# Small PSUM tiles for the attention's projections, constants as a scheduled job, and one engine for W z, in a convolution, attention and recurrence kernel

## The chip, the cores and the metric

The kernel runs on one core of a Trainium2 chip. The core has a matrix engine (TensorE, PE in the profile; PEld is its weight load), VectorE (DVE), ScalarE (ACT), GpSimd (POOL) and SyncE (SP), whose queue issues most of the transfers. The metric is the device time of one execution in microseconds, as the median of the runs shown.

## What is computed

The input x is 32 images of 128 channels and 64 x 64 pixels, all in 32-bit floats. Cut to what matters:

```python
x = x + dyn_conv3x3(group_norm(x))           # per image a kernel, mixed of four by softmax(sigmoid(.))
t = tokens(x)                                # (32, 4096, 128)
t = t + L1_attn(layer_norm(t))
t = t + L1_ffn(layer_norm(t))

def L1_attn(x):                              # windows of 144 tokens, stride 72, 4 heads of 4
    xb = x @ w_down.T + b_down               # 128 -> 16
    q, k, v = split(windows(xb) @ in_proj_w.T + in_proj_b)
    o = softmax(q @ k.T / 2) @ v @ out_proj_w.T + out_proj_b
    up = overlap_average(o) @ w_up.T + b_up  # 16 -> 128
    return layer_norm(x + sigmoid(gate) * up) * gamma + beta

def L1_ffn(x):
    z = batch_norm(x @ W.T)                  # over all images and tokens
    y[t] = sigmoid(z[t] + y[t - 1] @ V.T)    # a scan over 4096 tokens
    return y
```

## The kernel before

The program has two long stages. **The images** (`images`, up to L1150) take the 32 images through convolution, attention and the product with W. **The runs** (`by_runs`, L1603) do the scan.

The runs come only after the last image, since the normalisation of z takes its mean and variance over all of them. The scan of 4096 tokens is cut into 128 runs of 32 steps (RUN), and each run starts 20 steps early (WARM) from zero. Two images make a group, so one step works on 128 x 256 numbers. The 16 groups go through four streams in turn: a step is a product of `fVT` with the last y on PE into one of eight PSUM tiles `v`, the addition of scl times z, a sigmoid on ACT with the shift, and a copy of y into the place of z on POOL. `product` (L1632) does the addition in two ways. For five of six step numbers VectorE adds scl z to the PSUM tile (L1636); for the sixth PE multiplies z by the diagonal matrix `dgs` into the same tile first (L1638, L1639). A finished group is added onto the output in memory by a transfer that POOL issues (L1667), and then the load of the group six further on can follow, where its buffer is the same.

In the images, an order of work is written out when the program is built. Each image has eight generators (jobs): load, conv, project, feed, attend, divide in two halves, and tail. A job yields before each step with the engine that the step begins on, the PSUM pool that it needs, and the tiles that it reads. A planner (L1127) keeps a modelled clock for each engine and takes the first job, by due time, whose next step can begin no later than PE is free; if there is none, the one that can begin first. Convolution comes last in this order whatever its due time, so it fills what the others leave. Every engine then runs its own instructions strictly in the order written. The clock of the model is not the chip's; it only sets the order.

- load (L620): an image and its statistics; mixes the four kernels `k_d` by way of buffers `kx` into `wb`. The frames hold two images.
- conv (L698): transforms rows on POOL and VectorE (`ut`), multiplies on PE into `nm` tiles, and VectorE adds them to the frame.
- project (L753): layer norm into `zt`, and the down projection to 16 numbers per token: 32 matmuls into one `sc` tile, drained by one ACT instruction to `xb`, transposed by VectorE to `gt`.
- feed (L823): queries, keys and values from `gt`: qs and ks through one `sc` tile, Vc and VT through another. It waits until attention of the image before has read them all ("sets").
- attend (L888): 14 sets of windows, each in two halves; scores into an `sc` tile, exponentials by ACT, and the weighted sums of the half before into the tile `av`.
- divide (L996): sends the sums of the exponentials through small transfers to a layout in which VectorE inverts them (`cd`) and back; multiplies by `spr` on PE into an `sc` tile to spread them to all rows, scales `av`, and adds the up projection (`wc`) to `zt`. It runs for windows 0 to 3 and then for the rest.
- tail (L1066): the two layer norms and the product with W, and stores z.

[...] one `sc` tile of four banks, three `nm` tiles of one bank each, and one for `av`. A job that wants `sc` waits until whoever had it has drained all of it.

Ahead of the planner, the constants of the attention are made in a row: 52 small loads on SP, fills on POOL, copies on VectorE, and products on PE with `wuT` and others through `nm` tiles (L404 to L508). Before them come the loads of images 0 and 1 (L361) and the conversion of the four kernels to `k_d`.

Of the kernel before, what the change touches and what calls it, by code (L numbers as in the profile page):

```python
# [8 lines left out]
F32 = mybir.dt.float32  # L9
# [4 lines left out]
P = 128  # L14
EPS = 1e-5
H = W = 64
T = H * W
# [171 lines left out]
def hybrid_kernel(  # L189
# [153 lines left out]
    def images(nc):  # L343
# [6 lines left out]
        with ExitStack() as pa:  # L350
# [10 lines left out]
            for b in range(NF):  # L361
                fetch(b)


            with tc.tile_pool(name="gk", bufs=2) as gk:
                for k in range(NK):
# [11 lines left out]
                    nc.sync.dma_start(k_d[k], g4)  # L378
            keep = pa.enter_context(tc.tile_pool(name="keep", bufs=1))
# [23 lines left out]

            wqkv = []  # L404
            for i, n in enumerate(("wqB", "wkB", "wvB")):
                t = kept([P, P], n, 0.0)
                for g in range(NQ):
                    r = slice(16 * g, 16 * g + 16)
                    nc.sync.dma_start(t[r, r], in_projT[:, i * DK : (i + 1) * DK])
                wqkv.append(t)  # L410
            wqB, wkB, wvB = wqkv
            bqB, bkB = kept([P, 1], "bqB"), kept([P, 1], "bkB")
            bd = kept([P, 1], "bd", 0.0)
            wd2 = kept([P, 48], "wd2", 0.0)
            nc.vector.tensor_copy(wd2[:, DK : 2 * DK], wd[:, 0:DK])
            in_b1 = in_proj_b.rearrange("(c o) -> c o", o=1)
            for g in range(NQ):
                r = slice(16 * g, 16 * g + 16)
                nc.sync.dma_start(bqB[r], in_b1[0:DK])
                nc.sync.dma_start(bkB[r], in_b1[DK : 2 * DK])  # L420
            for g in range(NQ):
                nc.sync.dma_start(
                    bd[16 * g : 16 * g + DK], b_down.rearrange("(c o) -> c o", o=1)
                )

            mqk = kept([P, 2 * NH], "mqk")
            nc.vector.tensor_reduce(
                mqk, memb.rearrange("p (q g) -> p g q", q=4), axis=AX.X, op=ALU.add
            )

            m16 = kept([P, 8], "m16")
            nc.vector.tensor_reduce(
                m16, ident.rearrange("p (g k) -> p g k", k=16), axis=AX.X, op=ALU.add
            )
            mvt = kept([P, 2 * NH, HD], "mvt")
            nc.vector.tensor_copy(mvt, m16.rearrange("p (g o) -> p g o", o=1).to_broadcast([P, 2 * NH, HD]))

            VEs = []
            for i in range(2):
                v = kept([P, 4 * NH * NR + 32 - NR], f"VE{i}", 0.0)  # L440
                for h in range(NH):
                    nc.gpsimd.memset(
                        v[:, 0 : 4 * NH * NR].rearrange("p (q h o) -> p q h o", q=4, h=NH)[:, :, h, DK + h], 1.0
                    )
                VEs.append(v)
            Vc = kept([P, NWG * NQ * DK], "Vc")
            VTf = kept([P, NWG * NQ * NR + 32 - NR], "VT", 0.0)
            VT = VTf[:, 0 : NWG * NQ * NR].rearrange("p (w o) -> p w o", o=NR)
            for q in range(4):
                for u in range(2):  # L450
                    for m in range(NWG):
                        nc.vector.tensor_copy(
                            VT[:, NQ * m + 2 * q + u, DK:NR], mvt[:, NH * u : NH * (u + 1), 0]
                        )

            aw = kept([DK, NR], "aw")
            nc.sync.dma_start(aw[:, 0:DK], out_proj_w)
            bv = kept([DK, NH, HD], "bv")  # L460
            nc.sync.dma_start(
# [291 lines left out]
            def project(b):  # L753

                while ("conv", b) not in done:
                    yield
# [1039 lines left out]
```

## Time and profile before

| | us |
|---|---|
| median of 3 runs (lowest, highest) | 5605.47 (5600.29, 5619.85) |
| profiled execution, its time | 5616.06 |
| its span | 5614.3 |
| PE busy in the span | 4826.9 (86%) |
| DVE busy | 3636.3 (65%) |
| ACT busy | 2391.4 (43%) |
| POOL busy | 1606.5 (29%) |
| first matmul of a convolution | at 101 |
| last one | at 4664 |
| first step of the runs | at 4985 |

The span is the time from the first to the last instruction of one execution; the execution's own time is a little more. The page cuts the span into 40 slices and gives each engine's busy share in tenths (9 is 90% or more) and the granted PE clock:

```profile
PE   2897889989899898988988989989889897659996
DVE  4665666676666766766666766666676665347774
PEclk9998999999999999999999999999999999869998
```

PE is near full from the second slice on, falls off for two slices near the end of the images, and is full again in the runs, where VectorE and ACT are at seven tenths. A group row of the page has the line, engine, operation, tiles and shape, the number of instructions, and then busy time, mean length of one, and the engine's idle time before them with what ended it. Most of the images' instructions carry one line (L173), that of the wrapper which notes each operation for the model; so they are told apart by their tiles.

### The profile page before, as it was taken

The page shows a single profiled execution, that of the slowest core. Times are in us where ns is not written, and L with a number is a line of the kernel's source. Part 1 is how long each engine was busy: PE and PEld are TensorE (multiplying, and loading weights), DVE is VectorE, ACT ScalarE, POOL GpSimd, SP SyncE. Part 2 cuts the span into 40 slices and gives each one's busy share as a digit, 9 for nine tenths or more (in the row PEclk, how much of TensorE's full clock was granted, in tenths as well). Part 3 has the DMA queues.
Part 4 walks back from the last instruction along what each step waited for, and adds up shares of the span by engine and source line. Part 5 has one row for each costly group of instructions (what it writes and reads, how often), then busy time and mean ns, then how long its engine had stood idle before and what let it go on. Part 6 is the DMA issues. An engine that isn't in the chain of part 4 may idle for free. (4 is left out here: it accounts for less than half of the span.)

```text
span 5614.3 us, 105560 instructions
## 1 busy us (share of the span) xinstructions
PE 4826.9 (86%) x43707; PEld 2388.9 (43%) x43707; DVE 3636.3 (65%) x5044; ACT 2391.4 (43%) x3564; POOL 1606.5 (29%) x1561
## 2 busy tenths in 40 slices
PE   2897889989899898988988989989889897659996
PEld 1443444444444444444444444444444443326663
DVE  4665666676666766766666766666676665347774
ACT  0243444444344444434434433434444444327774
POOL 1331322222232222322322222222222221105664
PEclk9998999999999999999999999999999999869998
DMA  4534444454545545454444544544554444355997
GB/s 107 159 110 136 146 146 147 154 164 147 159 146 162 161 134 160 142 166 154 143 156 128 171 138 147 157 158 146 161 162 140 154 143 146 113 226 145 254 232 149
DMA packets 456796, 866.13 MB, mean 154 GB/s; under 512 B 297312, under 2 KB 307824, under 8 KB 423536
## 3 DMA queue, kind: packets, MB, share of 16 engines
q1 hardware_dynamic: 447600, 792.12, 44.3%
q0 software_dynamic: 8704, 67.11, 5.9%
q8 instruction: 350, 5.73, 0.4%
q14 instruction: 142, 1.16, 0.1%
HBM read 575.10 MB, written 275.78 MB: 152 GB/s over the span
## 5 line engine op out<-in xcount | busy, mean ns | idle before, releaser
L173 PE MATMUL nm<-ut,wb 128*128 128x512 f32 x3072 | 1599.6, 641 | 13.6 <-DVE wb L173 13.3
L173 ACT ACTIVATE ex<-sc 128x1152 f32<-128x1152 f32 x896 | 1013.6, 1131 | 1259.0 <-PE sc L173 1252.0
L173 PE MATMUL sc<-qe,ks 32*128 32x288 f32 x7168 | 722.5, 473 | 328.8 <-ACT ext L173 91.9
L173 POOL TENSOR_TENSOR qe<-qs,mqk 128x576 f32<-128x576 f32 x448 | 626.8, 1405 | 1316.2 <-PE sc L173 1292.3
L173 PEld LDWEIGHTS nm<-ut,wb 128*128 128x128 f32 x3072 | 538.2, 196 | 597.4 <-issue 584.8
L173 POOL TENSOR_TENSOR ut<-frames 128x576 f32<-128x576 f32 x384 | 538.9, 1433 | 870.1 <-PE nm L173 840.9
L173 DVE TENSOR_TENSOR frames<-frames,nm 128x512 f32<-128x512 f32 (+1 forms) x640 | 494.6, 791 | 290.1 <-PE nm L173 282.9
L173 PEld LDWEIGHTS sc<-qe,ks 32*128 32x128 f32 x7168 | 296.7, 190 | 875.4 <-issue 315.1
L173 PE MATMUL av<-ex,VE 128*32 128x144 f32 x14336 | 653.1, 302 | 2.6 <-DVE av L173 1.5
L173 PEld LDWEIGHTS av<-ex,VE 128*32 128x32 f32 x14336 | 372.2, 112 | 337.4 <-issue 269.3
L1635 PE MATMUL v<-yw,fVT 128*128 128x256 f32 (+1 forms) x1368 | 389.5, 417 | 73.3 <-ACT yw L1654 27.3
L1636 DVE SCALAR_TENSOR_TENSOR v<-zr,scl,v 128x256 f32<-128x256 f32 (+1 forms) x557 | 333.7, 654 | 138.3 <-PE v L1635 137.1
L173 DVE TENSOR_TENSOR zt<-zt,place 128x1024 f32<-128x1024 f32 x256 | 331.8, 1296 | 115.5 <-DMA place<-r_d 99.6
L173 DVE SCALAR_TENSOR_TENSOR wb<-kx,co,wb 128x768 f32<-128x768 f32 x192 | 243.3, 1267 | 141.9 <-DMA kx<-k_d 140.2
L1635 PEld LDWEIGHTS v<-yw,fVT 128*128 128x128 f32 x1368 | 234.2, 194 | 215.6 <-ACT yw L1663 96.8
L173 ACT ACTIVATE place<-zt 128x1024 f32<-128x1024 f32 x256 | 263.7, 1052 | 129.8 <-DVE zt L173 87.4
L173 DVE TENSOR_TENSOR place<-place 128x256 f32<-128x256 f32 x416 | 229.6, 552 | 137.5 <-ACT place L173 128.1
L1664 POOL COPY zr<-yw 128x256 f32<-128x256 f32 x416 | 261.4, 694 | 159.9 <-ACT yw L1663 159.7
L1663 ACT ACTIVATE yw<-v,shf 128x256 f32<-128x256 f32 x512 | 241.5, 475 | 129.8 <-DVE v L1636 67.3
L173 PE MATMUL nm<-place,avg 128*32 128x256 f32 x3072 | 250.4, 399 | 17.0 <-ACT place L173 15.2
L173 ACT COPY zt<-nm 128x512 f32<-128x512 f32 x256 | 150.1, 587 | 267.8 <-PE nm L173 267.7
L173 DVE SCALAR_TENSOR_TENSOR zt<-sc,gbc,zt 128x576 f32<-128x576 f32 (+1 forms) x192 | 175.4, 913 | 135.5 <-PE sc L173 135.3
(194 smaller groups left out, 5664.6 us busy)
## 6 DMA issues: line engine op xcount, KB each, us to landing
place<-r_d SPq DMA_DIRECT2D x512, 512.0 KB
kx<-k_d SPq DMA_DIRECT2D x256, 384.0 KB
x_d<-frames SPq DMA_DIRECT2D x32, 2112.0 KB
place<-x_d SPq DMA_DIRECT2D x128, 528.0 KB
frames<-in_x_dram SPq DMA_DIRECT2D x128, 512.0 KB
out_dram<-zt SPq DMA_DIRECT2D x64, 1024.0 KB
z_d<-zt SPq DMA_DIRECT2D x64, 1024.0 KB
zr<-z_d SPq DMA_DIRECT2D x26, 2048.0 KB
```

Of the source, the lines that this page charges most:

```text
L173: got = f(*args, **kw)
L1635: nc.tensor.matmul(ps, fVT, y, start=True, stop=True)
L1636: nc.vector.scalar_tensor_tensor(ps, z, scl, ps, ALU.mult, ALU.add)
L1663: nc.scalar.activation(yw[r % 2], ps, AF.Sigmoid, bias=shf)
L1664: nc.gpsimd.tensor_copy(zt[:, :, :, r], yw[r % 2])
```

## The change

- The down projection takes four `nm` tiles in turn, each drained by an ACT instruction of its own.
- Feed works in three parts, of windows 0 to 2, 3 to 5 and 6. Each part takes four `nm` tiles (q, k, values, values of the last 16 tokens) and starts when attention of the image before is past its windows. Attention starts after the first part and waits for the others at sets 6 and 12. `qs`, `ks` and `kt` get fixed places.
- The inverse sums take an `nm` tile for each of their three or two parts.
- Attention's wait for the second divide of the image before comes ahead of the set's copies instead of behind.
- The constants become a job of the planner with due time 0.5, which project waits for; image 1 is fetched behind the kernels' conversion.
- Due times: second divide from b - 0.15 to b + 0.6, project from b - 1.4 to b - 1.25, load from b - 2.8 to b - 2.5, feed from b - 1.2 to b - 0.9.
- In the runs every product is a matmul and a VectorE addition; `dgs` is gone.

```diff
@@ -358,8 +358,7 @@
                 for i in range(4):
                     nc.sync.dma_start(rows(xs[b % NF], 16 * i, 16), x[b, :, 16 * i : 16 * i + 16, :])
 
-            for b in range(NF):
-                fetch(b)
+            fetch(0)
 
 
             with tc.tile_pool(name="gk", bufs=2) as gk:
@@ -376,6 +375,8 @@
                     nc.vector.tensor_add(g4[:, 1], g4[:, 1], g3[:, :, 1])
                     nc.vector.tensor_scalar_mul(g4[:, 1:3], g4[:, 1:3], 0.5)
                     nc.sync.dma_start(k_d[k], g4)
+            for b in range(1, NF):
+                fetch(b)
             keep = pa.enter_context(tc.tile_pool(name="keep", bufs=1))
...
-            wqkv = []
-            for i, n in enumerate(("wqB", "wkB", "wvB")):
-                t = kept([P, P], n, 0.0)
...
+            wqB = wkB = wvB = bqB = bkB = bd = wd2 = mqk = mvt = VEs = Vc = VTf = VT = wc = fWc = gbc = avg = spr = None
...
             def project(b):
 
-                while ("conv", b) not in done:
+                while ("conv", b) not in done or "setup" not in done:
                     yield
                 xt = done["conv", b]
...
-                yield "PE", "sc", (zt[:, 0:T],)
 
                 xb = one.tile([P, 2, 4 * WIN], F32, name="xb")
-                ps = sc_tile()
                 for k in range(4):
                     n = 2 * WIN if k % 2 == 0 else WIN
+                    yield "PE", "nm", (zt[:, 0:T],)
+                    ps = nm_tile()
                     for v in range(2):
                         for q in range(4):
                             o = base[q] + GT * (k // 2) + 2 * WIN * (k % 2) + 4 * WIN * v
                             w = n if v else 2 * WIN
                             nc.tensor.matmul(
-                                ps[32 * q : 32 * q + 32, k, 0:w],
+                                ps[32 * q : 32 * q + 32, 0:w],
                                 wd2[:, DK * (1 - v) : DK * (3 - v)],
                                 zt[:, o : o + w],
                                 start=(v == 0),
                                 stop=(v == 1),
                             )
-                nc.scalar.activation(
-                    xb.rearrange("p u (k t) -> p (u k) t", k=2),
-                    ps[:, :, 0 : 2 * WIN],
-                    AF.Identity,
-                    bias=bd,
-                )
+                    nc.scalar.activation(
+                        xb.rearrange("p u (k t) -> p (u k) t", k=2)[:, k], ps[:, 0 : 2 * WIN], AF.Identity, bias=bd
+                    )
                 yield "DVE", None, (xb,)
...
-                done["gt", b] = zt, gt, gf, gtt
+                done["gt", b] = zt, gf, gtt
+            qs, ks = kept([P, GT], "qs"), kept([P, GT], "ks")
+            kt = kept([P, NWG, 2 * NH, 16], "kt")
 
             def feed(b):
 
-                while ("gt", b) not in done or (b and ("sets", b - 1) not in done):
-                    yield
-                zt, gt, gf, gtt = done["gt", b]
-                yield "PE", "sc", (gt,)
-                qs = one.tile([P, GT], F32, name="qs")
-                ks = one.tile([P, GT], F32, name="ks")
-                ps = sc_tile()
-                for i, wt in enumerate((wqB, wkB)):
-                    for c in range(2):
-                        n = 32 - c
+                for m0, m1 in ((0, 3), (3, 6), (6, NWG)):
+                    while ("gt", b) not in done or (
+                        b and (gone.get(("att", b - 1), 0) <= 4 * m1 if m1 < NWG else ("sets", b - 1) not in done)
+                    ):
+                        yield
+                    zt, gf, gtt = done["gt", b]
+                    t, n = slice(WIN * m0, WIN * m1), m1 - m0
+                    for wt in (wqB, wkB):
+                        yield "PE", "nm", (gf,)
+                        ps = nm_tile()[:, 0 : WIN * n]
+                        nc.tensor.matmul(ps, wt, gf[:, t], start=True, stop=True)
+                        if wt is wqB:
+                            nc.scalar.activation(
+                                qs[:, t].rearrange("p (m d r) -> p m d r", m=n, r=9),
+                                ps.rearrange("p (m r d) -> p m d r", m=n, r=9),
+                                AF.Identity,
+                                bias=bqB,
+                            )
+                        else:
+                            nc.scalar.activation(ks[:, t], ps, AF.Identity, bias=bkB)
+                    nc.gpsimd.tensor_mul(
+                        kt[:, m0:m1],
+                        ks[:, t].rearrange("p (m o t) -> p m o t", o=1, t=WIN)[:, :, :, P:WIN].to_broadcast(
+                            [P, n, 2 * NH, 16]
+                        ),
+                        mqk.rearrange("p (m g o) -> p m g o", m=1, o=1).to_broadcast([P, n, 2 * NH, 16]),
+                    )
+                    yield "PE", "nm", (gf,)
+                    ps = nm_tile()
+                    for m in range(m0, m1):
                         nc.tensor.matmul(
-                            ps[:, 2 * i + c, 0 : 16 * n],
-                            wt,
-                            gf[:, BLK * c : BLK * c + 16 * n],
+                            ps[:, P * (m - m0) : P * (m - m0 + 1)],
+                            gf[:, WIN * m : WIN * m + P],
+                            wvB,
                             start=True,
                             stop=True,
                         )
...
-                done["proj", b] = zt, qs, ks, kt
+                    nc.scalar.copy(Vc[:, P * m0 : P * m1], ps[:, 0 : P * n])
+                    yield "PE", "nm", (gtt,)
+                    ps = nm_tile()
+                    for m in range(m0, m1):
+                        nc.tensor.matmul(
+                            ps[:, P * (m - m0) : P * (m - m0 + 1)],
+                            gtt[:, m].rearrange("p g k -> p (g k)"),
+                            wvB,
+                            start=True,
+                            stop=True,
+                        )
+                    nc.vector.tensor_mul(
+                        VT[:, NQ * m0 : NQ * m1].rearrange("p (w u) o -> p w u o", u=2)[:, :, :, 0:DK],
+                        ps[:, 0 : P * n].rearrange("p (w u o) -> p w u o", u=2, o=DK),
+                        mvt.rearrange("p (w u h) f -> p w u (h f)", w=1, u=2).to_broadcast([P, n * 4, 2, DK]),
+                    )
+                    done["fed", b, m0] = True
+                done["proj", b] = zt
 
             av = kept([P, 2 * GT], "av")
 
             def attend(b):
 
-                while ("proj", b) not in done or (b and ("div", b - 1, 0) not in done):
+                while ("fed", b, 0) not in done or (
+                    b and (("sets", b - 1) not in done or ("div", b - 1, 0) not in done)
+                ):
                     yield
-                zt, qs, ks, kt = done["proj", b]
+                zt = done["gt", b][0]
...
                 for s in range(2 * NWG):
                     m, u = s // 2, s % 2
+                    while (b and s == 10 and ("div", b - 1, 1) not in done) or (
+                        s in (6, 12) and ("fed", b, m) not in done
+                    ):
+                        yield
                     o = m * WIN
                     v0 = VEs[s % 2]
...
-                    while b and s == 10 and ("div", b - 1, 1) not in done:
-                        yield
...
                         held = (s, ap, hp, ex, ext)
+                        gone["att", b] = 2 * s + hp + 1
...
-                yield "PE", "sc", (av[:, t],)
-                ps = sc_tile()
                 parts = 3 - d
                 n = n // parts
                 for c in range(parts):
                     o = slice(2 * WIN * m0 + n * c, 2 * WIN * m0 + n * (c + 1))
+                    yield "PE", "nm", (av[:, o],)
+                    ps = nm_tile()
                     for q in range(4):
                         r = slice(32 * q, 32 * q + NR + NH)
-                        nc.tensor.matmul(
-                            ps[32 * q : 32 * q + 32, c, 0:n], spr[r], av[r, o], start=True, stop=True
-                        )
-                av2 = av[:, t].rearrange("p (c t) -> p c t", c=parts)
-                nc.vector.tensor_mul(av2, av2, ps[:, 0:parts, 0:n])
+                        nc.tensor.matmul(ps[32 * q : 32 * q + 32, 0:n], spr[r], av[r, o], start=True, stop=True)
+                    nc.vector.tensor_mul(av[:, o], av[:, o], ps[:, 0:n])
...
-                zt = done["proj", b][0]
+                zt = done["proj", b]
...
+            def setup():
+                nonlocal wqB, wkB, wvB, bqB, bkB, bd, wd2, mqk, mvt, VEs, Vc, VTf, VT, wc, fWc, gbc, avg, spr
+                yield "SP", None, ()
+                wqkv = []
...
+                yield "DVE", None, (bv, aw)
+                nc.vector.tensor_mul(bv, bv, aw[:, 0:DK].rearrange("e (h f) -> e h f", f=HD))
...
+                yield "DVE", None, (bo, aw)
+                nc.vector.tensor_add(aw[:, DK : DK + 1], aw[:, DK : DK + 1], bo)
...
+                yield "PE", "nm", (aw, wuT)
+                wps = nm_tile()
+                wmn = kept([P, 1], "wmn")
+                for q in range(4):
+                    r = slice(32 * q, 32 * q + NR)
+                    nc.tensor.matmul(wps[r, 0:P], aw, wuT, start=True, stop=True)
+                    nc.vector.tensor_reduce(wmn[r], wps[r, 0:P], axis=AX.X, op=ALU.add)
+                    nc.vector.tensor_scalar_mul(wmn[r], wmn[r], 1.0 / P)
+                    nc.vector.tensor_scalar(
+                        wc[r], wps[r, 0:P], wmn[r], ghalf[r], ALU.subtract, ALU.mult
+                    )
+                yield "PE", "nm", ()
+                fcp = nm_tile()
...
+                done["setup"] = True
+            done, gone = {}, {}
             pa.enter_context(tc.manual_schedule())
-            jobs = []
+            jobs = [[False, 0.5, 0, setup(), None]]
             for b in range(NB):
                 for stage, g in enumerate(
                     (tail(b), divide(b, 0), divide(b, 1), attend(b), project(b), load(b), conv(b), feed(b))
                 ):
-                    jobs.append([stage == 6, b + (-0.05, -0.15, -0.15, 1.65, -1.4, -2.8, 0, -1.2)[stage], b, g, None])
+                    jobs.append([stage == 6, b + (-0.05, -0.15, 0.6, 1.65, -1.25, -2.5, 0, -0.9)[stage], b, g, None])
...
-            dg = hp.tile([P, P], F32, name="dgs")
-            nc.vector.tensor_scalar_mul(dg, ident, scl)
...
-            def product(ps, z, y, n):
-                if n % 6:
-                    nc.tensor.matmul(ps, fVT, y, start=True, stop=True)
-                    nc.vector.scalar_tensor_tensor(ps, z, scl, ps, ALU.mult, ALU.add)
-                else:
-                    nc.tensor.matmul(ps, dg, z, start=True, stop=False)
-                    nc.tensor.matmul(ps, fVT, y, start=False, stop=True)
 
...
-                            product(ps, z, yw[1 - r % 2][:, :, 1:], r + j)
+                            nc.tensor.matmul(ps, fVT, yw[1 - r % 2][:, :, 1:], start=True, stop=True)
+                            nc.vector.scalar_tensor_tensor(ps, z, scl, ps, ALU.mult, ALU.add)
                             nc.scalar.activation(y, ps, AF.Sigmoid, bias=shf)
                         yield
                     for r in range(RUN):
                         ps = p_v.tile([P, NI, NRUN], F32, name=f"v{j}")
-                        product(ps, zt[:, :, :, r], yw[1 - r % 2], r + j)
+                        nc.tensor.matmul(ps, fVT, yw[1 - r % 2], start=True, stop=True)
+                        nc.vector.scalar_tensor_tensor(
+                            ps, zt[:, :, :, r], scl, ps, ALU.mult, ALU.add
+                        )
                         nc.scalar.activation(yw[r % 2], ps, AF.Sigmoid, bias=shf)
                         nc.gpsimd.tensor_copy(zt[:, :, :, r], yw[r % 2])
                         yield
```

## The prediction

> **What bounds it.** I read the 40 slices first, then busy time by stage, then one stage at a time. The columns of the stage table are stretch, length, busy time of PE, PEld, DVE, ACT and POOL (instructions), granted clock, DMA share, GB/s.
>
> ```profile
> 101.00:400.00 299.00, 270.88 (x2134) 129.28 (x2138) 196.95 (x264) 89.11 (x123) 91.87 (x75) 0.96 0.39 119
> 400.00:4600.00 4200.00, 3741.84 (x36823) 1789.21 (x36820) 2815.72 (x3673) 1756.65 (x2396) 1119.93 (x871) 0.95 0.49 152
> 4600.00:4985.00 385.00, 255.55 (x2834) 124.86 (x2833) 181.22 (x238) 148.55 (x199) 46.16 (x38) 0.84 0.37 131
> 5034.00:5520.00 486.00, 473.64 (x1713) 302.28 (x1712) 360.99 (x648) 350.40 (x751) 297.28 (x484) 1.00 0.77 198
> ```
>
> PE bounds both long stages: 89% busy in the images (400 to 4600) and 97% in the runs (5034 to 5520). It hardly works before 101 us, and the last images (4600 to 4985) have too little for it. In the images only the 458 us of PE idle can be won. The PE groups there, the last field being idle time before them:
>
> ```profile
> L173 PE MATMUL nm<-ut,wb 128*128 128x512 f32 x2679 | 1411.6, 644 | 0.0
> L173 PE MATMUL sc<-qe,ks 32*128 32x288 f32 x6336 | 636.9, 472 | 280.7 <-ACT ext L173 76.4 <-POOL qe L173 60.8 <-ACT ex L173 49.7
> L173 PE MATMUL sc<-av,spr 24*32 24x384 f32 (+1 forms) x1144 | 163.1, 566 | 60.8 <-DMA av<-cd 59.1 <-ACT ex L173 1.6
> L173 PE MATMUL sc<-wvB,gt 128*128 128x128 f32 x392 | 56.7, 304 | 13.1 <-ACT ks L173 13.1
> L173 PE MATMUL nm<-mv,grp 128*128 128x1 f32 x56 | 12.6, 295 | 41.6 <-DVE mv L173 41.6
> ```
>
> The convolution never waits for a buffer (0.0), so where it is at hand it fills every hole; the idle time lies where attention runs without it.
>
> **Start, -14 us.** SyncE's queue (start, length, what):
>
> ```profile
> 53.33 0.32 SPq L378 DMA_DIRECT2D k_d<-g  x1
> ...
> 80.46 0.42 SPq L173 DMA_DIRECT2D wuT<-in_w_upT_dram  x1
> 94.71 4.59 SPq L173 DMA_DIRECT2D kx<-k_d  x3
> ```
>
> The 52 constant loads take SP from 56.7 to 80.9. PE then waits for wuT until 82.6, and the first image's statistics queue behind it: kx only goes on at 94.7, and the convolution is steady from 109.8. After the change the four fetches of image 1 (half of 16.6 us, 8.3) go behind the kernels, so SP's sum is the same and ends near 81. But the job gives way before its PE work, so the statistics (mv was ready at 27) are done by then, and kx follows at once: 94.7 - 80.9 = 14 saved. Bounds: 0 if the job's PE steps still come first; 38 if its loads fall behind all kx. The job issues its loads in one step ahead of kernel 2, so I take the 14. Its 60-odd DVE instructions (the VT copies take 4.1 us) and POOL fills fall into the time before k_d is written. Its four up-projection matmuls, each waiting some 1.9 us for DVE, now lie in that wait; uncovered they cost 6.
>
> **Images, -75 us.** The edits take 5 of 39 sc uses per image (down 1, feed 2, spr 2) to the nm tiles: 4 + 12 + 5 = 21 uses. The matmul columns stay the same. The order of due times within one turn was feed, both divides, tail, load, project; it becomes first divide, tail, feed, load, second divide, project. PE waits that belong to the moved drains: ks 13.1, and DVE VT (15.5 by the waits table) before the next scores: both go, 29. For the inverse sums PE waits 59.1 for the DMA, 17 times; nm doesn't bring the DMA sooner, but the second divide's later due time puts it, with the eight small transfers that it issues on SP (2.75 and 2.85 us per four), behind tail, feed and load; the tail of that image then starts later by about as much. I take half, 30; bounds 0 and 59. Feed now runs inside the previous attention. Before, qs, ks, kt on POOL, Vc and VT stood in a row, here 9.2 us from qs to the first exponential (timeline of one turn):
>
> ```profile
> 2712.64 1.10 ACT L173 ACTIVATE qs<-sc,bqB 128x1008 f32<-128x1008 f32 x1 [4.95 <-PE sc L173]
> ...
> 2721.83 1.13 ACT L173 ACTIVATE ex<-sc 128x1152 f32<-128x1152 f32 x1 [2.31 <-PE sc L173]
> ```
>
> What is late next there is project, which had gt only at 2881 for the following image, so the chain shortens in about two images of three. PE's share of this is the POOL qe wait, 60.8, of which half lies at the starts of images: 30. Sum 89.
>
> Added: ACT splits 1 to 4 and three times 1 to 3, 9 instructions more. ACT's copies of 64 and 512 columns (237, 587 ns) give 0.78 ns a column and 0.19 us fixed, so 1.7 us per image; DVE gains 5 (VT 2, spr 3) at about 0.17 and POOL 2, some 1 us each. All lie on engines 42%, 67% and 27% busy beside PE; uncovered they would cost 3.7 us x 32 = 118. Here a rule speaks against the change: **the Trainium skill**, Perfetto Trace Analysis, "Optimizing Scalar/DVE Operations", says that each ACT or DVE instruction has a fixed access cost and that larger operations pay when the engine is saturated. It gives ACT 51 ns on PSUM, 0.5 us per image instead of 1.7; ACT is not saturated, so neither figure reaches the end. The price that can reach PE is a late release of nm: 0.0 us over the convolution's 16 uses per image, but 9.3 us over 8 product uses in 28 images, 0.04 each. Half of that: 21 x 0.02 x 32 = 14. Net -75; bounds +80 (rival C) and -229 (half the idle). The wait for the second divide at s = 10, put ahead of VE and qe, holds up those two on ACT and POOL, then the scores behind them; the divide is done within 20 us of the previous attention's end, long before s = 10: nothing.
>
> **Last images, -9 us.** Nothing fills here: image 31's gt comes at 4783, its first exponential at 4803. A third of the feed is enough to start: some 5 us instead of 14.
>
> **Runs, -43 us.** One round (16 groups make four) is 131.85 us and 204 products. Its row by stage, DVE back to back, PE back to back in the chain of waits, and products with W z on PE:
>
> ```profile
> 5103.95:5235.80 131.85, 129.54 (x475) 84.10 (x474) 98.86 (x180) 96.91 (x209) 83.56 (x136) 1.00 0.90 229
> ```
> ```profile
> 5122.39 9.13 DVE L1636 SCALAR_TENSOR_TENSOR v<-zr,scl,v 128x256 f32<-128x256 f32 x16 [0.77 <-PE v L1635]
> ```
> ```profile
> 5087.43 9.15 PE v L1635 x34
> ```
> ```profile
> 5201.15 1.03 PE L1638 MATMUL v<-zr,dgs 128*128 128x256 f32 x2
> 5201.99 0.61 PE L1639 MATMUL v<-yw,fVT 128*128 128x256 f32 x2
> 5202.44 1.03 PE L1638 MATMUL v<-zr,dgs 128*128 128x256 f32 x2
> ```
>
> A product with dgs takes PE 5202.44 - 5201.15 = 1.29 us, a plain one 9.15/17 = 0.54 (34 records, two for each product). 170 x 0.54 + 34 x 1.29 = 136, about the round. After: PE at most 204 x 0.54 = 110; DVE's pitch is (9.13 - 0.65)/15 = 0.565, so 204 x 0.565 = 115 and DVE is the bound. The same page of the skill would give DVE 125 ns on PSUM beside 256 columns at 0.96 GHz (VectorE: DVE Perf Modes, "Specifications"): 0.39, 80 us a round, and -110 for the stage. The row decides, and at 97% busy a round is 119. A lone stream takes 2.46 us a step at half clock, under 2.0 at full clock: 52 steps are 104, below 119. DMA:
>
> ```profile
> q0 software_dynamic: 2176, 16.78, 63.2%
> q1 hardware_dynamic: 908, 13.30, 26.1%
> ```
>
> A store takes 0.632 x 131.85/4 = 20.8 us, a load about 10: 31 per group against 29.8. A group's store and the load that waits for it must end two groups later, at 60 us. Over ten loads they fall 12 us behind, with 60 - 31 = 29 to spare, so DMA doesn't bind. Saved: 12.9 x 486/131.85 = 48. Where one or two streams run alone, a dgs step took 1.77 us instead of 2.46, without DVE; some seven of those come back: +5.
>
> **Sum.** -14 - 75 - 9 - 43 = -141. The profiled execution took 5616.06 (span 5614.3): 5475. The median of the runs is 10.6 lower: 5605.47 - 141 = 5464, say 5465.
>
> **Rivals.** A, the images stay (25%): conv fills what the feed leaves, and the PE waits move instead of going; for it, 89% busy PE; against it, 29 us of waits lose their cause. -66, 5540. B, the images gain more (16%): attention without gaps halves the 458 idle; for it, attentions of 113 to 127 us in a period of 149 us (qs rows of images 6 to 29); against it, 41.6 us waits for mv, untouched. -229 - 66: 5310. C, slower (6%): the nm tiles become the wait. Three serve convolution, product, deviations and now 21 uses more, drained by in-order DVE and ACT; at the deviations' 0.34 us a use (12.5 + 1.4 + 15.0 over 3 uses in 28 images) that is 228 us against 89 + 66 gained: +73, 5680. It decides from 0.23 us a use; the 0.0 of the convolution speaks against it. D, DVE takes its full 0.65 us per product (8%): 133 a round, runs +10 instead of -43: 5518. The 16 in a row speak against it. My forecast keeps 45%.
>
> **How the numbers follow.** Its own range is 5420 to 5520; A and D reach to 5560, B down to 5360 for part of its chance: 5360 to 5570. A measurement tells apart about 0.3%, 17 us. Faster: forecast, A, B and D less 3%: 0.91; slower: C, 0.06; same 0.03.
>
> **What would show it.** Convolution steady near 95 us; no PE wait for ks or VT; the scores' idle time below 240; "nm<-ut,wb" still near 0.0; rounds of 119 us with DVE at 97% and PE near 85%. Wrong if PE waits at nm, if attention's gaps stay near 30 us, or if a round is over 128.

## The result, and the profile after

| | before | after |
|---|---|---|
| median (lowest, highest), us | 5604.6 (5600.29, 5619.85) | 5547.35 (5532.06, 5552.78) |
| ratio, 95% interval | | 0.9889 [0.9862, 0.9916] |
| profiled execution, its span | 5616.06, 5614.3 | 5545.78, 5544.0 |
| first convolution matmul at | 101 | 92 |
| from there to the last one | 4563 | 4570 |
| from there to the first step of the runs | 324 | 295 |
| the runs | 627 | 587 |

The change takes off 57 us, not 141. By the traces (70 us between the spans) the start gives 9, the convolution part -7, the last images 29 and the runs 40. The runs are counted from the first sigmoid on. Both image terms together are 22 where the prediction had 84.

The slices of the page after, in tenths:

```profile
PE   3898888979989889898898988998988988749995
DVE  5656765666766667676676666676666765448995
PEclk9998999989999999999999999999999999869997
```

The middle looks as before. Only the runs, the last slices, show a change: VectorE is now full there. The stages, with columns as in the prediction:

```profile
101.00:400.00 299.00, 276.95 (x2259) 132.31 (x2259) 181.12 (x257) 99.33 (x150) 92.26 (x79) 0.93 0.34 102
400.00:4600.00 4200.00, 3741.42 (x36926) 1799.82 (x36928) 2780.42 (x3845) 1804.58 (x2649) 1085.39 (x929) 0.95 0.49 153
5080.00:5180.00 100.00, 98.07 (x352) 52.78 (x352) 99.16 (x183) 84.47 (x179) 69.93 (x116) 1.00 0.96 248
5180.00:5280.00 100.00, 95.37 (x341) 50.93 (x340) 96.95 (x178) 82.29 (x175) 69.98 (x115) 1.00 1.03 283
```

From 400 to 4600, PE is busy 3741.42 us against 3741.84: as idle as before. What it waits for is not the same. PE groups after, 400 to 4600, the last field being the idle time:

```profile
L173 PE MATMUL nm<-ut,wb 128*128 128x512 f32 x2714 | 1389.9, 633 | 9.7 <-DVE wb L173 9.0
L173 PE MATMUL sc<-qe,ks 32*128 32x288 f32 x6300 | 631.7, 471 | 204.4 <-ACT ext L173 81.5 <-ACT VE L173 64.8 <-POOL qe L173 34.9
L173 PE MATMUL av<-ex,VE 128*32 128x144 f32 x12592 | 570.3, 301 | 21.8 <-DVE av L173 21.8
L173 PE MATMUL nm<-place,avg 128*32 128x256 f32 x2720 | 215.0, 394 | 34.7 <-ACT place L173 33.9
L173 PE MATMUL nm<-av,spr 24*32 24x384 f32 (+1 forms) x1144 | 164.2, 589 | 134.6 <-DMA av<-cd 134.4
L173 PE MATMUL nm<-wvB,gt 128*128 128x128 f32 x392 | 66.3, 300 | 9.2 <-ACT qs L173 7.1 <-ACT ks L173 1.4
L173 PE MATMUL nm<-zt,avg 128*32 128x256 f32 x928 | 65.8, 400 | 24.7 <-DVE zt L173 24.7
L173 PE MATMUL nm<-mv,grp 128*128 128x1 f32 x56 | 11.0, 265 | 0.0
```

Gone are the waits for ks and VT (29), for mv (41.6) and 26 of the 60.8 for qe; the scores' idle time fell from 280.7 to 204.4. Some 12 us come back in feed, where the next matmul now waits until ACT or VectorE has drained an `nm` tile (8.8 of it for qs; the row of `wvB,gt` has 9.2). New are 75 us at the inverse sums (59.1 to 134.4), and some 54 at `av`, `place` and `zt`. The one large loser is the wait for `av<-cd`, which the prediction had put on the winning side.

What stands there is read from SyncE's queue and from PE, here around the second divide of image 10. SyncE sends `av`'s sums out (`cd<-av`, here at 1815.72) and the inverses back (`av<-cd`). Its queue after (start, length, what; the last number counts the transfers in the row):

```profile
1836.06 0.32 SPq L173 DMA_DIRECT2D z_d<-zt  x1
1836.48 9.53 SPq L173 DMA_DIRECT2D frames<-in_x_dram  x4
1846.06 2.82 SPq L173 DMA_DIRECT2D kx<-k_d  x2
1848.99 3.02 SPq L173 DMA_DIRECT2D av<-cd  x4
```

PE after, in the same stretch:

```profile
1843.17 0.70 PE L173 MATMUL av<-ex,VE 128*32 128x144 f32 x16
1843.68 0.43 PE L173 MATMUL av<-ext,VT 128*32 128x144 f32 x8
1853.84 3.59 PE L173 MATMUL nm<-av,spr 24*32 24x432 f32 x16 [9.73 <-DMA av<-cd]
```

VectorE had the inverses ready at 1839.0. But SyncE was busy issuing the fetch of the next image, 9.53 us for four transfers, and two kernels behind it, and got to `av<-cd` at 1848.99. PE, in the order written, stood 9.73 us. The planner books 0.6 us of SyncE for a transfer, so to it this place looked free. The stall has a tail, which the stages hide. Stretches of PE after: length, busy time, granted clock, DMA share, GB/s:

```profile
1849.00:1853.00 4.00, 0.00 (x0) 0.50 0.94 259
1853.00:1856.00 3.00, 2.16 (x13) 0.50 0.04 9
1856.00:1859.00 3.00, 3.00 (x24) 0.50 0.00 0
1859.00:1862.00 3.00, 3.00 (x22) 0.51 0.02 5
1862.00:1866.00 4.00, 4.00 (x16) 1.00 0.00 0
```

PE works for 8 us at half clock before it is granted the full one: some 4 us lost on top of the 9.7, an estimate from this table. Over all images PE waits 149.7 us for `av<-cd` after, 133 of them in 16 stalls of over 3 us, 14 of these in second divides; before, it waits 67.5, of which 60 in 8 such stalls. (The expectations below put the two sums at 146 and 69.) In all of them but the last of each kernel, a fetch and two kernels stand between the ready inverses and their transfer: 15 times after, 7 times before.

### The profile page after: what moved, and what is told of

Same layout as the page of the kernel before. It is cut to its first block, busy times and chain, and to the rows that moved or that the text cites. A ratio compares the mean times of both kernels' runs of the same rounds, so it can differ in the third digit from the quotient of the medians.

```text
span 5544.0 us, 106009 instructions
## 1 busy us (share of the span) xinstructions
PE 4768.8 (86%) x43571; PEld 2315.6 (42%) x43571; DVE 3648.5 (66%) x5335; ACT 2453.1 (44%) x3852; POOL 1569.2 (28%) x1625
## 4 chain that ended last, share of the span: by engine, by line
PE 47%; DVE 21%; DMA 14%; ACT 7%; issue 4%; SPq 3%; POOL 2%; DVEq 0%; ACTq 0%; POOLq 0%
PE nm L173 30%; PE sc L173 10%; DVE zt L173 6%; PE av L173 5%; DMA place<-r_d 4%; DVE v L1665 4%; DMA kx<-k_d 3%; ACT ex L173 3%; SPq L173 3%; DMA av<-cd 2%; DVE v L1659 2%; ACT place L173 2%; DVE place L173 2%; DVE frames L173 2%; DVE wb L173 1%
## 5 line engine op out<-in xcount | busy, mean ns | idle before, releaser
L173 PE MATMUL nm<-ut,wb 128*128 128x512 f32 x3072 | 1566.2, 633 | 16.8 <-DVE wb L173 15.6
L173 POOL TENSOR_TENSOR qe<-qs,mqk 128x576 f32<-128x576 f32 x448 | 586.8, 1315 | 1364.1 <-PE sc L173 1332.8
L173 DVE SCALAR_TENSOR_TENSOR wb<-kx,co,wb 128x768 f32<-128x768 f32 x192 | 231.6, 1206 | 217.6 <-DMA kx<-k_d 215.9
L1664 PE MATMUL v<-yw,fVT 128*128 128x256 f32 x1024 | 327.0, 442 | 43.3 <-ACT yw L1668 42.1
L173 PE MATMUL nm<-av,spr 24*32 24x384 f32 (+1 forms) x1280 | 193.2, 600 | 149.9 <-DMA av<-cd 149.7
L173 DVE TENSOR_TENSOR place<-place 128x256 f32<-128x256 f32 x416 | 217.3, 522 | 150.8 <-ACT place L173 141.3
L1665 DVE SCALAR_TENSOR_TENSOR v<-zr,scl,v 128x256 f32<-128x256 f32 x416 | 254.9, 655 | 43.7 <-PE v L1664 43.7
L173 DVE TENSOR_TENSOR av<-av,nm 128x384 f32<-128x384 f32 (+1 forms) x160 | 89.7, 570 | 260.6 <-PE nm L173 258.2
```

The costliest lines, as they stand in the source:

```text
L173: got = f(*args, **kw)
L1664: nc.tensor.matmul(ps, fVT, yw[1 - r % 2], start=True, stop=True)
L1665: nc.vector.scalar_tensor_tensor(ps, zt[:, :, :, r], scl, ps, ALU.mult, ALU.add)
```

## The experiments

Theories. **S**: the fetch in the middle of a divide, with its tail of half clock, is what the images' gain was lost to. **N**: the inverse sums hold `nm` tiles too early. **M**: stalls only move, and each order written is a draw of luck. Formed later: **R**, the order that the hold happens to give is what helps, whatever the change; and **P**, what counts is how evenly the order spaces the images.

Each ratio is to the kernel before on the same chip, over all executions, so it isn't the quotient of two medians; the last column is (ratio - 1) x 5605 us. By it the change is worth 62 us.

| run | median, us | ratio, interval | us |
|---|---|---|---|
| after | 5547.35 | 0.9889 [0.9862, 0.9916] | -62 |
| runs_only | 5542.75 | 0.9916 [0.9885, 0.9946] | -47 |
| start_only | 5609.74 | 0.9991 [0.9977, 1.0005] | -5 |
| due_div | 5617.3 | 1.0052 [1.0028, 1.0076] | +29 |
| fetch_pool | 5499.19 | 0.9821 [0.9786, 0.9856] | -100 |
| hold | 5288.78 | 0.9447 [0.9414, 0.948] | -310 |
| before_hold | 5603.62 | 0.9979 [0.9969, 0.9988] | -12 |
| hold_lag | 5591.7 | 0.9964 [0.9952, 0.9977] | -20 |
| hold_due | 5563.07 | 0.992 [0.9895, 0.9945] | -45 |
| hold_spr | 5596.08 | 0.9979 [0.9967, 0.9991] | -12 |
| after_even | 5550.07 | 0.9918 [0.9901, 0.9935] | -46 |
| after_pairs | 5798.86 | 1.0371 [1.0353, 1.0388] | +208 |
| before_even | 5715.74 | 1.0226 [1.0209, 1.0243] | +127 |
| sp_model | 5448.0 | 0.9746 [0.973, 0.9762] | -142 |
| defer | 5446.22 | 0.9699 [0.968, 0.9719] | -169 |
| before_defer | 5635.68 | 1.0044 [1.0028, 1.0061] | +25 |

**runs_only** is the kernel before with the runs of the change (`dgs` and its products out, every product a matmul and an addition).

> The kernel before with the runs alone changed (every product a matmul and a VectorE addition). Its images are in the old order. By the prediction the runs save 43 us (a round of 119 instead of 131.85 us): 5562. By the rival with VectorE at 0.65 us per product they lose 10: 5615. If the DMA binds once the rounds are shorter, the saving is 20 to 35: 5570 to 5585.

47 us, and in its trace the runs take 585 us instead of 627: the runs' term is right by itself, since the images keep the order of before.

**start_only** is the kernel before with the constants as a job, due 0.5, and `fetch(1)` behind the kernels' conversion.

> The kernel before with the start's edits alone (constants as a job with due time 0.5, fetch of image 1 behind the kernels' conversion). The order of the middle images repeats as in before. By the first convolution's start in the trace of after (101 to 92 us): 8 to 9 faster, against the 14 of the prediction; if the phase of the images shifts with it, anything within 60.

The first convolution starts at 91 instead of 101. The 10 us can't be told from nothing in the median (the interval holds 1); the trace carries this term.

**due_div** takes back the due time on which the prediction's term for the inverse sums rests:

```diff
-(-0.05, -0.15, 0.6, 1.65, -1.25, -2.5, 0, -0.9)
+(-0.05, -0.15, -0.15, 1.65, -1.25, -2.5, 0, -0.9)
```

> The changed kernel with the second divide's due time back at b - 0.15, ahead of load in the order. Theory S, with the due time as the reason that more fetches fall between the transfers: the wait for av<-cd falls from 149.7 us to 60 to 90 us, and the time by 40 to 80 us. If the due time is not the reason, the wait stays above 110 us.

Slower, and over all images PE still waits 122.4 us for `av<-cd` (after: 149.7). From 400 to 4600 it waits 102.7 in 37 places against 134.4 in 26. But the fetch now stands between the halves of 9 divides, about every third image, where after has 15 and before 7; those nine stalls take 59 us, the fifteen 123. The other waits are short (3.5 us at most) and have no fetch in them. So with the due time back the fetch leaves some of the gaps, as the prediction's step has it, though not all. That the time rose can't be put down to this edit alone, as the whole order is another.

**hold** lets no load start while a divide is under way:

```diff
                     or (b >= NF and ("frame", b - NF) not in done)
+                    or gone.get("cd", 0)
                 ):
...
+                gone["cd"] = gone.get("cd", 0) + 1
                 yield "DVE", None, (cd,)
...
+                gone["cd"] -= 1
                 parts = 3 - d
```

> The changed kernel, except that a load doesn't start its fetch (and first two kx) while a divide has sent cd and not yet av. Theory S (the second divide's return transfers stand behind the next image's fetch, 9.5 us, on SP's queue, and PE waits for them): PE's wait for DMA av<-cd falls from 149.7 us to below 60, and the time by 60 to 110 us against the changed kernel, to 5440 to 5490. Theory N (the inverse sums' matmuls come too early because an nm tile is free where the sc tile was not): the wait stays above 110 us and the time within 20 us of 5547. Theory M (PE is full anyway, waits only move): the wait falls, but others grow by as much, and the time stays within 20 us of 5547.

**fetch_pool** leaves the order as it is and lets GpSimd issue the fetch:

```diff
+                q = nc.sync if b < NF else Queue(nc, "SP", nc.nc.gpsimd)
                 for i in range(4):
-                    nc.sync.dma_start(rows(xs[b % NF], 16 * i, 16), x[b, :, 16 * i : 16 * i + 16, :])
+                    q.dma_start(rows(xs[b % NF], 16 * i, 16), x[b, :, 16 * i : 16 * i + 16, :])
```

> The changed kernel with the fetches of images 2 to 31 issued from POOL's queue, while the order of all other work on every engine stays as in the changed kernel. Theory S: with SP free of the fetch the wait for av<-cd falls below 50 us, some of it comes back as POOL waits (qe late), time 5450 to 5510. Theory N: the wait stays above 110. Theory M: the wait falls and the time stays within 20 us of 5547 with other PE waits grown.

fetch_pool takes the wait from 134 to 41 us (400 to 4600) and gains 38; issuing on GpSimd costs there (qe's wait goes from 31 to 51, 400 to 4350). hold gains 248 over after, far more than S can explain with 150 us of stalls and their tails. So the next four runs asked whether the hold itself was the reason. **before_hold** has the same hold in the kernel before; **hold_lag** is hold with the planner's assumed delay between engines (`LAG`) at 0.06 instead of 0.05; **hold_due** has the old due times; **hold_spr** the inverse sums through one `sc` tile.

> The kernel before with the same hold: a load does not issue its fetch and first two kx while a divide has sent its sums and not yet sent the inverses. Theory S (the fetch standing in SP's queue between the two halves of a divide, with the half clock that follows each stall of PE, is what the change gave back): the kernel before had 69 us of such stalls (63 in the second divide, 6 in the first), with about half as much again in clock, so about 5500 here, and what the image and start edits are worth without the block is this less 47 (the runs) less hold's 5289, about 160. Theory R (the hold helps by the regular order that it happens to give, whatever the change): it gives here what it gave there, 250, so about 5345, and the image edits are worth nothing. Theory M (stalls only move): within 30 of 5593.

> hold with the planner's assumed delay between engines at 0.06 us instead of 0.05: no instruction is added or dropped, only the order can differ. Theory S: the stall at the inverse sums stays below 25 us and the time within 40 of hold's 5289. Theory M (each order is a draw of luck): more than 60 away.

> hold with all four due times as before the change (second divide b-0.15, project b-1.4, load b-2.8, feed b-1.2), the edits themselves kept. If the new due times carry the gain in the images: well above hold, 5400 or more. If the small tiles and the three parts carry it: within 40 of 5289.

> hold with the inverse sums through one sc tile as before the change (the five nm uses of an image gone, two sc uses back). Theory N (the nm tiles are the cost): faster than hold by 20 to 60. Theory S: the product waits for the transfer in either pool, and while it waits it holds the one sc tile and the scores behind it, so slower than hold by 10 to 60.

As reasons for hold's gain, S and R both fail here. In all four the stalls over 3 us at the inverse sums are mostly gone (8, 25, 39 and 13 us), and none is near hold. hold_lag, which differs from hold by a constant in the planner, lies 300 above it. Its idle time (400 to 4350) is 413 us against hold's 306: it waits 59 for VE where hold has 27, 53 at `place` (35) and 32 for qe (10). hold_spr gains nothing by leaving the `nm` tiles, as N would have it, but beside hold it can't be read as an effect of its edit, since the order is another. Every one of these edits shifts modelled times, and with them the whole order on all engines. The order of hold repeats itself for every image, that of before after three, that of after after five. Is that it? **after_even** and **after_pairs** are after with `LAG` at 0.08 and 0.07; **before_even** is before at 0.07. **sp_model** gives the planner SyncE's own times:

```diff
-            return 0.6, 2.5 + (1.2e-5 if run >= 128 else 4e-5) * n * int(out.ap[0][1])
+            took = 2.5 + (1.2e-5 if run >= 128 else 4e-5) * n * int(out.ap[0][1])
+            busy = 0.4 if n * int(out.ap[0][1]) < 40000 or run > 1000 else 1.35 if run >= 128 else 2.4
+            return busy, took + busy
```

> The kernel after with the planner's assumed delay between engines at 0.08 us instead of 0.05 and nothing else: the order written out then starts the attentions of the middle images at equal distances and repeats itself for every image, where the kernel after repeats only after five (distances 131, 128, 155, 135, 135 on the planner's clock), the kernel before after three (136, 160, 124), and hold for every image. Theory P (what bounds the images is how evenly the order spaces them; uneven orders lose what the edits save, whatever stall they are freed of): near hold, 5290 to 5400. Theory S (only the fetch in the middle of the divides): after's 5547 less or more what the divide's stalls come to here, 60 us of stalls left would give about 5450. Theory M (hold was a lucky draw and evenness has nothing to do with it): 5500 to 5620, as hold_lag.

> The same with the delay at 0.07: the order repeats after two images, at distances of 158 and 126 on the planner's clock. Theory P: no better than after, 5520 to 5620, so 150 or more above after_even. Theory M: within 60 of after_even, on either side.

> The kernel before with the delay at 0.07 and nothing else: its order too repeats for every image. Theory P alone (evenness is all, the image edits nothing): as much faster than before as after_even is than after, some 200 to 250. If the edits pay only once the order is even: a gain well below that of after_even, under 150. Theory M: 5540 to 5640.

> The kernel after with the planner told what the trace shows of SyncE: a fetch piece holds it 2.4 us, a kx piece 1.35, the others 0.4, instead of 0.6 each. Its order repeats for every image, without the hold. Theory P: near hold, 5290 to 5400, even where the divides still stall. Theory S: near hold only if the stalls at the inverse sums fall under 30 us. Theory M: 5500 to 5620.

P falls: after_even repeats for every image and is no faster than after; before_even does so too and is 127 us slower than before. What stays is that one constant of the model moves this kernel by 250 us (after_even to after_pairs), so that a comparison in which the order changes, hold's among them, shows no more than two draws. sp_model, with prices of the queue near the measured ones, is 80 better than after, and its stalls over 3 us at the inverse sums are down to 12.5; but it too has another order.

The comparison that is free of this changes SyncE's queue alone. **defer** books the fetch and the first two `kx` in the planner where they were, and issues them behind the inverses:

```diff
+                def issue(out, src):
+                    if gone.get("cd", 0):
+                        nc.note("SP", "dma_start", (out, src), {})
+                        late.append((out, src))
+                    else:
+                        nc.sync.dma_start(out, src)
...
+                gone["cd"] -= 1
+                if not gone["cd"]:
+                    send_late()
```

PE, VectorE, ScalarE and GpSimd have the same instructions in the same order as in after (in the traces, row for row but for 4 of PE's 43571). **before_defer** is the same on before. What was open by then: how much of the missing gain is the fetch, and how much the order.

> The kernel after; where a load would issue its fetch or first two kx inside an unfinished divide, SyncE issues them right behind the inverses instead (the planner books them where it did, so PE, VectorE, ScalarE and GpSimd keep the order of after row for row). Theory S (the block is what ate the images' gain, 146 us of stalls over 3 us and the half clock behind them): the stalls fall under 50 us and the time by 60 to 120, to 5430 to 5490. Theory M (what is won at one wait is waited at the next even in a fixed order): 5510 or more with the stalls gone.

> The same on the kernel before, order of the four engines kept. It had 69 us of such stalls against 146. Theory S: 30 to 70 faster than before, about half of what defer gains on after, so that without the block after lies about 100 below before, of which 48 are the runs and 9 the start. Theory M: within 20 of before.

defer gains 0.019 of the time over after, 107 us. Its queue at the same second divide of image 10, and its group rows, 400 to 4600:

```profile
1800.05 0.32 SPq L173 DMA_DIRECT2D z_d<-zt  x1
1802.99 2.70 SPq L173 DMA_DIRECT2D av<-cd  x4
1805.79 8.09 SPq L520 DMA_DIRECT2D frames<-in_x_dram  x4
1813.94 2.55 SPq L520 DMA_DIRECT2D kx<-k_d  x2
```
```profile
L173 PE MATMUL nm<-av,spr 24*32 24x384 f32 (+1 forms) x1160 | 138.8, 511 | 8.3 <-DMA av<-cd 8.0
L173 PE MATMUL nm<-mv,grp 128*128 128x1 f32 x56 | 13.2, 306 | 46.0 <-DVE av L173 33.4 <-DVE frames L173 12.2 <-DVE VT L173 0.4
```

The inverses are sent as soon as VectorE has them (1803.0), PE's wait falls from 134.4 to 8.0, and 46 us come back at the statistics, whose image now arrives later. With the order fixed, S is shown: 126 us of waits less, 46 more, 107 us of time. In the traces the convolution part falls by 92 us, from 4570 to 4478: 75 of it is idle time of PE (485 to 410), and 17 is busy time, the same matmuls with 420 us at half clock instead of 495. N falls with this: the inverse sums take `nm` tiles as in after, and the wait is gone. fetch_pool points the same way, for there too PE, VectorE and ScalarE keep the order of after. In before_defer the same rows read:

```profile
L173 PE MATMUL sc<-av,spr 24*32 24x384 f32 (+1 forms) x1120 | 155.2, 557 | 11.6 <-DMA av<-cd 9.8 <-ACT ex L173 1.8
L173 PE MATMUL nm<-mv,grp 128*128 128x1 f32 x56 | 14.1, 320 | 111.5 <-DVE mv L173 111.5
```

Here the wait of 59.1 falls to 9.8, but that for mv grows from 41.6 to 111.5, and the kernel is 25 us slower. S had expected 30 to 70 us of gain; in the order of before, PE needs the fetched image's statistics next, and the stall only moves, as M has it. Where the fetch may wait is a property of the order around it.

Of all these, hold is the fastest, 310 us below before. Neither has the block, so that hold beats defer by some 140 us must lie in its order; hold_lag shows that orders differ by that much, not what in the order does it. Its row of 400 to 4350 and that of after (columns as in the stage table):

```profile
400.00:4350.00 3950.00, 3644.29 (x37049) 1765.25 (x37046) 2782.22 (x3859) 1807.13 (x2658) 1092.62 (x930) 0.98 0.51 164
```
```profile
400.00:4350.00 3950.00, 3520.66 (x34586) 1690.96 (x34584) 2610.89 (x3603) 1686.98 (x2476) 1013.90 (x867) 0.94 0.49 153
```

In hold PE idles 306 us of this, in after 429, and the granted clock is 0.98 against 0.94. It has 7 gaps of PE over 3 us where after has 32, and 181 us at half clock where after has 440. sp_model, which repeats for every image too, also has 7 such gaps, but idles 384 us and has 273 at half clock. What makes hold's order so much better stays open.

## Why the prediction was right and wrong

**What bounds it**: right. Where a convolution is in progress it fills PE; over all seventeen kernels (700 to 4350), PE idles 2.5% to 9% of the time between a convolution's first and last matmul and 22% to 33% of the rest. After stands highest in the first number, 9.0%; with the fetch deferred it is 7.0%. PE takes its instructions in the order written, so a product that waits for `av<-cd` holds up the convolution behind it, as above.

**Start, -14**: -9 by the trace, the right way and mis-sized. kx went on 12 us earlier (82.6 instead of 94.7), but VectorE stood on the small steps of the four up-projection products from 82.7 to 88.5 and mixed the kernels behind them: the 6 us that they would cost "uncovered" were not covered.

**Images, -75, and last images, -9**: here it failed. Right were the waits for ks and VT (29 predicted, 29 gone) and for qe (30 predicted, 26 gone). Of the 14 for a late release of `nm`, 12 came, in feed itself (8.8 for the drain of qs, 1.7 for ks, 1.3 for VT and Vc); the convolution's 9.7 us is a wait for `wb`. Unforeseen were mv, -42, called untouched, and some +54 at `av`, `place` and `zt`, rival A's mechanism. The step that failed is "nm doesn't bring the DMA sooner, but the second divide's later due time puts it [...] behind tail, feed and load [...] I take half, 30; bounds 0 and 59". The wait grew by 75 instead, to 134.4, with both ends of the bounds on the wrong side. Being behind load means that the load's fetch is behind `cd<-av` and ahead of `av<-cd` in one queue. The term counted the divide's own eight transfers (2.75 and 2.85 us per four) and the delay of the tail, but not the 9.5 us of the four that the load puts into that gap. How much of it the due time alone does stays open: with it put back, due_div has the fetch in 9 gaps instead of 15, not in 7. The profile of before held the answer: 51 of its 59.1 us were stalls of over 3 us behind the same block, in every third image, here before a stall of 7.3 us:

```profile
2845.73 2.76 SPq L173 DMA_DIRECT2D cd<-av  x4
2848.59 8.20 SPq L173 DMA_DIRECT2D frames<-in_x_dram  x4
2856.84 2.62 SPq L173 DMA_DIRECT2D kx<-k_d  x2
2859.56 2.69 SPq L173 DMA_DIRECT2D av<-cd  x4
```

With the block deferred and nothing else changed, the convolution part and the last images come to 4478 + 299 = 4777 us against 4563 + 324 = 4887 before: 110 gained where 84 were forecast. The one term cost some 107. That the other terms then come out about right in sum may be luck: the order is new as well, no run separates these terms, and such a sum is known to some 35 us only (runs_only, with its images in the order of before, takes 4530 + 321 = 4851).

**Runs, -43**: right; -40 by the trace, -47 alone (-42 in that trace). A round, predicted 119, is 119 to 121 us in the middle of the stage (5110 to 5300), with VectorE at 97% to 99%. PE reads 95% to 98% where 85% were expected; why it reads so high was not looked into. By the access cost that the prediction cites from **the Trainium skill**, Perfetto Trace Analysis, "Optimizing Scalar/DVE Operations", a round would have been 80, an estimate; the measured round is half as long again. The "-110 for the stage" that stands beside it doesn't follow from 80: 52 us a round are some 190 over the stage, and PE, at most 110 a round by the prediction's own sum, would have held it at some 80. That a lone stream takes under 2.0 us a step at full clock is an estimate (2.46 less half of the 1.21 that a product takes at half clock); no row here shows it.

**Rivals.** The time lies where A put it (5540), inside the range stated, and waits did move (54 us, at `av`, `place` and `zt`). But the larger loss, 75, is not what A had in mind: it is a new stall with a cause of its own, which defer takes out. C was wrong: its `nm` waits are 12 us, not 228. D was wrong: 119 a round, not 133. B's size is real, as hold shows (-310 in all against B's -295), but for the order, not for an attention without gaps.

## What to carry to other kernels

When a change moves one step past another in a written order, list what each puts into the shared transfer queue, with the queue's measured time for it, and look for a pair of transfers that now has a long issue between its halves. Where a planner writes the order, compare versions in which only the thing in question differs in the order, or run one with a constant of the planner nudged: the spread of those nudges is the error of every other comparison. What a queue costs belongs in the planner's model; here 0.6 us was booked for an issue that takes 2.0 to 2.4.

## What was not expected of the hardware

**The tail of a stall.** In all seventeen traces (400 to 4350) I counted PE's gaps that stand alone (no other over 0.5 us in the 15 us before and the 6 after), and whether the clock went to one half by 6 us after their end. After gaps of 3 us and more it did in 170 of 170; of 2 to 3 us in 119 of 154; of 1.5 to 2 us in 48 of 97; of 1 to 1.5 us in 18 of 175. The clock stayed at one half after the gap for a median of 3.4 us where the gap was 3 to 5 us long, and of 7.8 us after longer ones. **The Trainium skill**, TensorE: Matmul & The Clock Gate, "HAM oscillation — how this bites in real kernels", has the rule as no PE idle gaps above about 3.4 us; here gaps of 2 to 3 us were already followed by half clock in three cases of four. Of a stall's price, then, only the first part is in the idle column.

**The fetch's issue.** One of its four transfers takes SyncE 2.0 to 2.4 us (8.09 / 4 in defer, 9.53 / 4 in after) where one of `av<-cd` takes 0.7 (3.02 / 4) and one of kx 1.4 (2.82 / 2), in the lines above.
